# Two projections exchanged, one folding of sums and the loads of x moved, in a fused attention kernel

## The chip, the cores and the metric

The kernel runs on one core of one Trainium2 chip. The metric is the device time of one execution in microseconds (us). The kernel before takes 1832.31 us, the median of 3 runs (1831.64 to 1833.32).

## What is computed

For x of shape (32, 256, 32, 32) in float32, with S = 32 x 32 = 1024 tokens per batch element, the reference computes a group normalization, a causal attention with 8 heads of 32 channels that leaves out the diagonal, and a residual addition:

```
xn = gn(x)                                # 32 groups of 8 channels
q  = q_w @ xn + q_b;  kv = kv_w @ xn + kv_b
k, v = kv[:, :256], kv[:, 256:]           # each to (B, 8 heads, S, 32)
scores = q k^T / sqrt(32);  scores = where(mask == 0, -10000, scores)
attn   = softmax(scores);   attn   = where(mask == 0, 0, attn)
x = x + (attn v)                          # mask = tril(ones, -1)
```

## The kernel before, in words

The program is written out in full for 32 batches. A batch has two groups `g` of four heads (128 channels), and each group has six visits, so a batch has N = 12 visits, 0 to 11. The main loop (L700 to L717) runs over all 384 visits. Step i of it issues, in this order: the scores of visit i (`scores`, L339: products of k and q on TensorE into three PSUM tiles `sT`, exponentials on ScalarE into `e` and `eh`, and on GpSimd the masking of the blocks on the diagonal, `mask`, L320, into `diagonal`); the steps listed for i in `at`; then `values` (L399) and `add_keys` (L421) of visit i - 1, which are the products of the exponentials with v on TensorE into `acc`, and the running sums of the exponentials on VectorE; then the steps listed for i in `after`. Where the text says that something is done after visit i, step i of this loop is meant. A period of the loop, 12 steps, is one batch.

Which key blocks a visit needs is written in `PRODUCTS` (L566): visit 2 needs blocks 0 and 1, visit 3 blocks 2, 6 and 7, visit 4 blocks 4, 6 and 5. `projections` (L268) lists twelve pieces of projection per batch in order: eight of q and k (`project_qk`, tiles `pp`) and four of v (`project_v`, tiles `ppv`). Piece n of v, n = 0 to 3, makes the key blocks 2n and 2n + 1, and ends with a copy on ScalarE (L266). `PROJECT` (L621) gives each of the twelve pieces its step relative to the first visit of its batch, -5 to 6, in `at`; places 8 and 9 of the list, which hold v's pieces 2 and 3, go to steps 3 and 4.

Around these pieces other steps are placed by hand:

- `prepare` (L609) with `PREPARE` (L622) places the ten steps of a batch's normalization in `after`: statistics of the two channel groups (`norm_channels`, L172), `norm_mean` (L180, product `pm`), `norm_deviation` (L188, tile `dev` on VectorE), `norm_variance` (L200, product `pv` on `dev`), `norm_rstd`, and the four applications. They stand relative to the batch's first visit, so that -16 is visit 8 of the batch two before, and -9 and -8 are visits 3 and 4 of the batch just before.
- `SUMS` (L623) places the folding of the four sums of exponentials per batch. Sum n is first folded from 128 to 64 partitions (`fold`, L436: a DMA of 512 KB, issued by GpSimd, that adds one half of the tile to the other) in step SUMS[n], then from 64 to 32 (256 KB) two steps later, both in `after`, and is stacked (`stack`, L442: a plain DMA of 256 KB issued by SyncE) four steps after the first, in `at`. A step above 11 lies in the next batch. Sums 0 and 2 lie in `diagonal` tiles, sums 1 and 3 in `e` tiles. In step N + 8 the inverted sums are written to memory and read back into `rb` by four DMAs of 256 KB (`invert`, L485).
- `finish` (L519) divides, adds bias and residual on VectorE and stores each quarter of the output, in steps N + 13 (twice), N + 14 and N + 15.
- The loads of x, four of 256 KB per batch, are listed in `at` (L674).

TensorE, ScalarE, VectorE and GpSimd execute their instructions in the order in which this program issues them. On SyncE's queue, which carries the loads, the stackings, the inverses and the stores, a scheduler decides on the order: before the change it is, from visit 7 of one batch to visit 6 of the next: the stacking of sum 0, the write of the previous batch's inverses and the four reads of `rb`, the stackings of sums 1 and 2, the previous batch's four stores, one load of x, the stacking of sum 3, three loads. An instruction waits there for what it needs, and everything behind it waits too.

Of the kernel before, what the change touches and what calls it, by code (L numbers as in the profile page):

```python
# [32 lines left out]
def tile_norm_attention_residual(  # L33
# [24 lines left out]
    NH = S // HALF  # L58
# [40 lines left out]
    def unshifted():  # L99
# [4 lines left out]
        def load_part(b, g, cols):  # L104
            if (g, cols.start) == (0, 0):
                live["x", b] = xpool.tile([P, NG, S], F32, tag="x", name=f"x_{b}")
            nc.sync.dma_start(out=live["x", b][:, g, cols], in_=x_in[b, :, g, cols])
# [129 lines left out]
        def project_qk(b, g, n, hf):  # L237

            key = ("qk"[n], b, g)
            if hf == 0:  # L240
                live[key] = qkpool.tile([P, S], F32, tag="qk"[n], name=f"{'qk'[n]}_{b}_{g}")
            cols = slice(hf * HALF, (hf + 1) * HALF)
            pp = spare(f"pp_{b}_{g}_{n}_{hf}")
            for cc in range(NG):
                product(
                    pp, wT[:, cc, n * C + g * P : n * C + (g + 1) * P], live["xn", b, hf][:, cc, :],
                    start=cc == 0, stop=cc == NG - 1,
                )
            nc.scalar.activation(  # L249
                live[key][:, cols], pp, AF.Identity, bias=qk_bias[:, n, g : g + 1], scale=(SCALE, 1.0)[n],  # L250
            )

        def project_v(b, n):


            if n == 0:
                live["v", b] = work.tile([P, NB, C], F32, tag="v", name=f"v_{b}")
            pp = spare(f"ppv_{b}_{n}").rearrange("p (s c) -> p s c", c=C)
            hf, at = divmod(2 * n * P, HALF)
            for s in range(2):  # L260
                tokens = slice(at + s * P, at + (s + 1) * P)
                for cc in range(NG):
                    product(
                        pp[:, s, :], live["xn", b, hf][:, cc, tokens], wT[:, cc, 2 * C : 3 * C], start=cc == 0, stop=cc == NG - 1,
                    )
            nc.scalar.copy(live["v", b][:, 2 * n : 2 * n + 2, :], pp)  # L266

        def projections(b):  # L268

            qk = [[lambda g=g, hf=hf, n=n: project_qk(b, g, n, hf) for n in range(2)] for g in range(NG) for hf in range(NH)]  # L270
            v = [lambda n=n: project_v(b, n) for n in range(NB // 2)]
            return qk[0] + v[:1] + qk[1][:1] + v[1:2] + qk[1][1:] + qk[2] + v[2:] + qk[3]

# [160 lines left out]
        def fold(b, n, rows):  # L436
            total = live["sum", b, *divmod(n, NH)]
            if (n, rows) == (1, HD):
                nc.gpsimd.drain()
            nc.gpsimd.dma_start(out=total[:rows], in_=total[rows : 2 * rows], accum_op=ALU.add)  # L440

        def stack(b, n):  # L442
            if n == 0:
                live["folded", b] = work.tile([P, 4, HALF], F32, tag="folded", bufs=1, name=f"folded_{b}")
            total = live.pop(("sum", b, *divmod(n, NH)))
            nc.sync.dma_start(out=live["folded", b][n * HD : (n + 1) * HD], in_=total[:HD])

        def sum_folded(b, heads):
            if heads.start == 0:
                live["rows", b] = small.tile([P, ROW], F32, tag="rows", name=f"rows_{b}")  # L450
            for j in heads:
                turned = small.tile([P, HALF], F32, tag="turned", bufs=1, name=f"turned_{b}_{j}")
                nc.vector.transpose(turned, live["folded", b][:, j, :])
                nc.vector.tensor_reduce(
                    live["rows", b][:, j * HALF // HD : (j + 1) * HALF // HD],
                    turned.rearrange("p (k r) -> p k r", r=HD), AX.X, ALU.add,
                )
# [27 lines left out]
        def invert(b):  # L485
            rows = live["rows", b]
            check(rows, SUM_MIN, SUM_MAX)
            inv = small.tile([P, ROW], F32, tag="inv", name=f"inv_{b}")
            nc.vector.reciprocal(inv, rows)
            turned = small.tile([P, ROW], F32, tag="inv_turned", name=f"inv_turned_{b}")  # L490
            nc.vector.transpose(turned, inv)

            spread = dram.tile([2, 4, 2, HALF], F32, tag="inv", name=f"inverses_{b}")
            nc.sync.dma_start(
                out=spread.rearrange("a n j (m c) -> (n j m) a c", c=HD), in_=turned.rearrange("p (a c) -> p a c", a=2),
            )
            live["rb", b] = work.tile([P, 4, HALF], F32, tag="rb", bufs=1, name=f"rb_{b}")
            for h in range(4):
                nc.sync.dma_start(
                    out=live["rb", b][h * HD : (h + 1) * HD],  # L500
                    in_=spread[h // 2, :, h % 2, :].unsqueeze(0).broadcast_to([HD, 4, HALF]),
                )
# [60 lines left out]
        N, TOTAL = NG * len(VISITS), 2  # L563
# [42 lines left out]
        def when(i, f, where=at):  # L606
            where.setdefault(i, []).append(f)

        def prepare(b, whens):  # L609
            for n, f in zip(whens, [  # L610
                lambda: norm_channels(b, 0), lambda: norm_channels(b, 1), lambda: norm_mean(b),
                lambda: norm_deviation(b), lambda: norm_variance(b), lambda: norm_rstd(b),
            ] + [lambda hf=hf, g=g: norm_apply(b, hf, g) for hf in range(NH) for g in range(NG)]):
                if n is None:
                    f()
                else:
                    when(n, f, after)
# [1 line left out]


        PROJECT = (-5, -4, -3, -2, -1, 0, 1, 2, 3, 4, 5, 6)  # L621
        PREPARE = (-16, -15, -9, -9, -8, -8, -7, -6, -5, -3)  # L622
        SUMS = (3, 7, 9, 13)  # L623
        FINISH = (N + 13, N + 13, N + 14, N + 15)
        every = range(4)

        with tc.manual_schedule(engines={ENG.PE, ENG.Activation, ENG.DVE, ENG.Pool}):
# [38 lines left out]
            for b in range(B):  # L666
                first, last = b * N, b == B - 1
                if b >= 1:
                    for n, f in zip(PROJECT if not last else PROJECT[:-1] + (7,), projections(b)):
                        when(first + n, f)  # L670
                if b >= 2:
                    for n in range(NG * NH):
                        cols = slice(n % NH * HALF, (n % NH + 1) * HALF)
                        when(max(first - 2 * N + 4 + n, 0), lambda b=b, n=n, cols=cols: load_part(b, n // NH, cols))  # L674
                    prepare(b, [first + n for n in PREPARE])
                if not last:
                    for n in every:
                        v = first + SUMS[n]
                        when(v, lambda b=b, n=n: fold(b, n, 2 * HD), after)
                        when(v + 2, lambda b=b, n=n: fold(b, n, HD), after)  # L680
                        when(v + 4, lambda b=b, n=n: stack(b, n))
                    late = b == B - 2
                    v = first + N + (5 if late else 6)
                    when(v, lambda b=b: sum_folded(b, every[:2]), after)
                    when(v + 1, lambda b=b: sum_folded(b, every[2:]), after)
                    when(v + 2, lambda b=b: invert(b))
                    for n in every:
                        v = first + (N + 9 + n // 2 if late else FINISH[n])
                        when(v, lambda b=b, n=n: finish(b, n), after)
                else:  # L690
                    when(first + 3, lambda: sums(0, SUMMED[1], False), after)
                    when(first + 7, lambda: sums(1, SUMMED[5], False), after)
                    when(first + 9, lambda: sums(2, SUMMED[7], False), after)
                    when(first + 8, lambda b=b: invert_here(b, 0))
                    when(first + 9, lambda b=b: finish(b, 0))
                    when(first + 8, lambda b=b: invert_here(b, 1))
                    when(first + 8, lambda b=b: finish(b, 1))
                    when(first + 10, lambda b=b: invert_here(b, 2))
                    when(first + 11, lambda b=b: finish(b, 2), after)
            for i in range(B * N + 1):  # L700
# [4 lines left out]
                b, v = divmod(i - 1, N)  # L705
# [21 lines left out]
    def shifted():  # L727


        with ExitStack() as inner:  # L730
# [34 lines left out]
            with tc.For_i(0, B, 1) as b:  # L765
# [93 lines left out]
                )  # L859

    outside = unshifted()
    again = nc.values_load(outside[0:1, 0:1], min_val=0, max_val=P)
    with tc.If(again > 0):
# [26 lines left out]
```

## Time and profile before

| what | value |
|---|---|
| median of 3 runs | 1832.31 us |
| the profiled execution's own time | 1834.49 us |
| span of the profiled execution, from first to last instruction | 1832.8 us |
| granted TensorE clock | 0.998 |
| TensorE products (PE) | 1800.6 us busy |
| VectorE (DVE) | 1642.0 us busy, 90% |
| ScalarE (ACT) | 1456.2 us busy, 79% |
| GpSimd (POOL) | 842.1 us busy, 46% |
| DMA queue of GpSimd's folds (q0) | 97.53 MB, 36.0% of 16 engines' span |
| DMA queue of SyncE (q1) | 133.96 MB, 27.3% |
| instruction queue (q8) | 291 packets, 4.77 MB, 1.1% |

A line of a timeline gives start and duration in us, the engine, the line of the kernel, the operation, the tile written and those read, the shape, and a count of merged instructions. A bracket at its end tells how long the engine was idle before and what ended that. A line of the waits gives the waiting instruction, what it waited for, the total in us, how often, and the longest. PE is TensorE's products, PEld its loading of weights. "issue" means a wait for nothing that the profile shows. A line of DMA queues gives the kind of queue, its packets, MB, and the share of the time of 16 DMA engines in the stretch. Names of tiles stand without batch and buffer numbers.

### The profile page before, as it was taken

To read this page: it belongs to the slowest core of one execution; us is meant where nothing else is said; L and a number is where in the kernel's file an instruction comes from. 1 tells how busy PE (TensorE), PEld (TensorE's weight loads), DVE (VectorE), ACT (ScalarE), POOL (GpSimd) and SP (SyncE) were. 2 spreads that over 40 slices of the span, in tenths; PEclk is the share of its full clock that TensorE was granted. 3 is DMA by queue.
4 is the path that set the end of the run, shared out by engine and by line. 5 is a ranking of instruction groups with operands and counts; after the bars stand their busy time and mean duration, and the time that the engine had idled before them with its cause. 6 is when DMAs were issued, how large, how long until landed. Compare 5 with 4: busy or idle time off the path is not lost.

```text
span 1832.8 us, 81736 instructions
## 1 busy us (share of the span) xinstructions
PE 1800.6 (98%) x37036; PEld 958.2 (52%) x37036; DVE 1642.0 (90%) x1832; ACT 1456.2 (79%) x1985; POOL 842.1 (46%) x901
## 2 busy tenths in 40 slices
PE   9999999999999999999999999999999999999997
PEld 5555555555555555555555555555555555555553
DVE  4688999999998998999999999999998999999987
ACT  6778778888778887787887888877878778888774
POOL 2444544545544454445454454554444544545531
PEclk9999999999999999999999999999999999999999
DMA  3456676776766766666667666666666676766662
GB/s 122 72 101 136 128 142 122 136 151 120 145 124 129 144 135 126 132 132 135 143 128 148 116 135 147 127 137 126 138 135 130 132 142 124 136 146 124 123 123 74
DMA packets 86531, 236.79 MB, mean 129 GB/s; under 512 B 21280, under 2 KB 22304, under 8 KB 70304
## 3 DMA queue, kind: packets, MB, share of 16 engines
q0 software_dynamic: 15872, 97.53, 36.0%
q1 hardware_dynamic: 70304, 133.96, 27.3%
q8 instruction: 291, 4.77, 1.1%
q14 instruction: 64, 0.52, 0.1%
HBM read 66.85 MB, written 34.57 MB: 55 GB/s over the span
## 4 chain that ended last, share of the span: by engine, by line
PE 92%; ACT 6%; issue 1%; DVE 1%; DMA 0%; POOL 0%
PE sT L302 30%; PE pp L162 26%; PE acc L409 26%; PE ppv L162 10%; ACT e L384 3%; ACT eh L380 2%; ACT v L266 1%; PE pd L461 0%; DMA x<-in_x_dram 0%; PE pv L162 0%; DVE st L177 0%; PE pm L162 0%; POOL diagonal L330 0%; DVE rb_last L526 0%; DVE rb_last L514 0%
## 5 line engine op out<-in xcount | busy, mean ns | idle before, releaser
L384 ACT ACTIVATE e<-sT 128x1024 f32<-128x1024 f32 x768 | 745.6, 1022 | 263.1 <-PE sT L302 262.9
L330 POOL TENSOR_SCALAR_AFFINE_SELECT diagonal<-eh 128x512 f32<-128x512 f32 x512 | 541.6, 1081 | 777.9 <-ACT eh L380 777.8
L302 PE MATMUL sT<-q,k 32*64 32x128 f32 (+2 forms) x18432 | 587.7, 372 | 4.7 <-issue 4.4
L427 DVE TENSOR_TENSOR e<-e,e 128x1024 f32<-128x1024 f32 x315 | 541.9, 1720 | 19.5 <-ACT v L266 3.2
L302 PEld LDWEIGHTS sT<-q,k 32*64 32x64 f32 x18432 | 405.6, 131 | 188.8 <-PE sT L302 59.5
L162 PE MATMUL pp<-xn,wT 128*32 128x512 f32 x4096 | 493.2, 598 | 1.3 <-ACT e L384 1.1
L409 PE MATMUL acc<-e,v 128*32 128x384 f32 (+3 forms) x4608 | 402.0, 450 | 0.0
L380 ACT ACTIVATE eh<-sT 128x768 f32<-128x768 f32 (+1 forms) x384 | 341.0, 888 | 0.0
L409 PEld LDWEIGHTS acc<-e,v 128*32 128x32 f32 x4608 | 149.7, 110 | 261.1 <-issue 238.1
L162 PE MATMUL ppv<-wT,xn 128*32 128x256 f32 x4096 | 247.5, 382 | 0.0
L162 PEld LDWEIGHTS pp<-xn,wT 128*32 128x32 f32 x4096 | 107.8, 109 | 200.1 <-issue 165.6
L427 DVE TENSOR_TENSOR diagonal<-diagonal,e 128x1536 f32<-128x1536 f32 x126 | 188.0, 1492 | 25.7 <-PE acc L409 10.6
L427 DVE TENSOR_TENSOR e<-e,eh 128x1024 f32<-128x1024 f32 x127 | 171.5, 1351 | 6.9 <-ACT q L249 0.5
L409 PEld LDWEIGHTS acc<-diagonal,v 128*32 128x32 f32 x4096 | 119.5, 110 | 108.6 <-issue 97.1
L409 PE MATMUL acc<-diagonal,v 128*32 128x128 f32 x4096 | 160.4, 273 | 12.5 <-ACT v L266 12.5
L427 DVE TENSOR_TENSOR e<-e,diagonal 128x2048 f32<-128x2048 f32 x62 | 142.1, 2292 | 24.1 <-POOL diagonal L330 20.7
L162 PEld LDWEIGHTS ppv<-wT,xn 128*32 128x32 f32 x4096 | 120.4, 109 | 79.6 <-issue 7.2
L427 DVE TENSOR_TENSOR e<-e 128x512 f32<-128x512 f32 x64 | 66.9, 1046 | 80.3 <-PE acc L409 79.6
L526 DVE SCALAR_TENSOR_TENSOR rb<-num,v_bias_col,x 128x256 f32<-128x256 f32 x248 | 133.5, 579 | 4.4
L235 ACT ACTIVATE xn<-x,shift,rstd 128x256 f32<-128x256 f32 x248 | 137.2, 613 | 0.0
L440 POOL DMA_DIRECT2D diagonal<-diagonal x124 | 120.0, 968 | 32.9 <-DMA diagonal<-diagonal 32.4
L440 POOL DMA_DIRECT2D e<-e x124 | 102.3, 825 | 38.1 <-PE sT L302 34.8
(78 smaller groups left out, 1077.0 us busy)
## 6 DMA issues: line engine op xcount, KB each, us to landing
diagonal<-diagonal POOLq DMA_DIRECT2D x62, 512.0 KB, 8.9
e<-e POOLq DMA_DIRECT2D x62, 512.0 KB, 5.7
rb<-inverses SPq DMA_DIRECT2D x124, 256.0 KB, 4.7
out_dram<-rb SPq DMA_DIRECT2D x124, 256.0 KB, 5.0
x<-in_x_dram SPq DMA_DIRECT2D x120, 256.0 KB, 6.0
diagonal<-diagonal POOLq DMA_DIRECT2D x62, 256.0 KB, 4.7
folded<-diagonal SPq DMA_DIRECT2D x62, 256.0 KB, 3.5
e<-e POOLq DMA_DIRECT2D x62, 256.0 KB, 5.4
```

The source lines that it names most:

```text
L162: nc.tensor.matmul(out[part], lhsT=lhsT[:, part], rhs=rhs, start=start, stop=stop, skip_group_check=True)
L235: nc.scalar.activation(to, of, AF.Identity, bias=live["shift", b][:, g : g + 1], scale=rstd)
L266: nc.scalar.copy(live["v", b][:, 2 * n : 2 * n + 2, :], pp)
L302: return nc.tensor.matmul(bank[c : c + KEYS, cols], lhsT=live["k", b, g][rows, kb * P + c : kb * P + c + KEYS], rhs=live["q", b, g][rows, ...
L330: nc.gpsimd.affine_select(out=square[:, :, place + s * P : place + (s + 1) * P], in_=raw[:, :, (1 - s) * KEYS : (3 - s) * KEYS], pattern=[ ...
L380: exp = nc.scalar.activation(eh.rearrange("p (n bank) q -> p bank n q", n=2)[:, :, :, :narrow], short[:, :, :, :narrow], AF.Exp)
L384: nc.scalar.activation(e[:, 2 * a : 2 * a + 2, :wide], pairs[a][:, :, :wide], AF.Exp)
L409: nc.tensor.matmul(acc[HD * j : HD * (j + 1), of], lhsT=live["v", b][:, kb, h * HD : (h + 1) * HD], rhs=e[:, j, :], start=first, stop=last ...
L427: nc.vector.tensor_add(to, to, tile_of(b, g, at))
L440: nc.gpsimd.dma_start(out=total[:rows], in_=total[rows : 2 * rows], accum_op=ALU.add)
L526: nc.vector.scalar_tensor_tensor(blocks(rb, s), blocks(num, s, s == 1), v_bias_col[:, g : g + 1], blocks(xt[:, g, cols], s), ALU.add, ALU.add,
```

## The change

A slice, three numbers and a formula are edited. In the list of projections v's pieces 2 and 3 exchange places, so that piece 3 (key blocks 6 and 7) is made in step 3 and piece 2 (blocks 4 and 5) in step 4. The statistics of x move from -16 and -15 to -14 and -13, from visits 8 and 9 to 10 and 11. The folding of sum 2 moves from step 9 to 11, and with it its second fold from 11 to 13 and its stacking from 13 to 15; steps 13 and 15 are visits 1 and 3 of the next batch. The four loads of x are listed in steps 7, 7, 7 and 8 of the batch two before instead of 4, 5, 6 and 7.

```diff
-            return qk[0] + v[:1] + qk[1][:1] + v[1:2] + qk[1][1:] + qk[2] + v[2:] + qk[3]
+            return qk[0] + v[:1] + qk[1][:1] + v[1:2] + qk[1][1:] + qk[2] + v[:1:-1] + qk[3]
...
-        PREPARE = (-16, -15, -9, -9, -8, -8, -7, -6, -5, -3)
-        SUMS = (3, 7, 9, 13)
+        PREPARE = (-14, -13, -9, -9, -8, -8, -7, -6, -5, -3)
+        SUMS = (3, 7, 11, 13)
...
-                        when(max(first - 2 * N + 4 + n, 0), lambda b=b, n=n, cols=cols: load_part(b, n // NH, cols))
+                        when(max(first - 2 * N + 7 + n // 3, 0), lambda b=b, n=n, cols=cols: load_part(b, n // NH, cols))
```

As built, the order on GpSimd's queue differs only in the two folds of sum 2: the first stands behind the mask of visit 11 instead of behind the second fold of sum 1 in visit 9, the second between the mask of visit 1 and the first fold of sum 3. On SyncE's queue the stacking of sum 2 stands behind the first two stores instead of ahead of all four, and the four loads of x stand together behind the stacking of sum 3.

## The prediction

> **What bounds the kernel now.** I read the page first (busy shares and the chain), then the waits of TensorE, then its timeline in one batch, then VectorE's timeline of the same stretch, last the DMA queues.
>
> ```profile
> PE 1800.6 (98%) x37036; PEld 958.2 (52%) x37036; DVE 1642.0 (90%) x1832; ACT 1456.2 (79%) x1985; POOL 842.1 (46%) x901
> ...
> PE 92%; ACT 6%; issue 1%; DVE 1%; DMA 0%; POOL 0%
> ```
>
> TensorE is busy for 98% of the span and holds 92% of the chain. A change that removes no products can only take away TensorE's stalls, so I list these.
>
> ```profile
> PE acc L409 <- ACT v L266: 12.5, 32, 0.4
> PE sT L302 <- issue: 4.4, 5, 1.8
> ```
>
> The first row is the wait that the exchange of the projections is about: in each of the 32 batches the products of visit 3 wait for ScalarE's copy of the projection issued just ahead of them. The second row has no releaser. Matmul ends are modelled, so I price stalls by distances of starts. TensorE's timeline of two visits with the same products (visit 9 of batch 15 without, visit 3 of batch 16 with the wait; then `pv`, norm_variance):
>
> ```profile
> 913.34 1.04 PE L409 MATMUL acc<-e,v 128*32 128x512 f32 x8
> 914.20 0.62 PE L409 MATMUL acc<-diagonal,v 128*32 128x128 f32 x16
> ...
> 940.97 1.04 PE L409 MATMUL acc<-e,v 128*32 128x512 f32 x8
> 942.40 0.64 PE L409 MATMUL acc<-diagonal,v 128*32 128x128 f32 x16 [0.39 <-ACT v L266]
> 942.83 0.25 PE L162 MATMUL pv<-dev,avg 128*32 128x2 f32 x8
> ```
>
> The start distance is 0.86 us without and 1.43 us with the wait: it costs 0.57 us. VectorE in the same stretch:
>
> ```profile
> 932.90 3.09 DVE L427 TENSOR_TENSOR diagonal<-diagonal,e 128x1536 f32<-128x1536 f32 x2 [0.27 <-issue]
> ...
> 936.63 1.69 DVE L526 SCALAR_TENSOR_TENSOR rb<-num,v_bias_col,x 128x256 f32<-128x256 f32 x2
> ...
> 941.29 0.88 DVE L526 SCALAR_TENSOR_TENSOR rb<-num,v_bias_col,x 128x256 f32<-128x256 f32 x2
> ...
> 942.47 0.16 DVE L197 TENSOR_TENSOR dev<-dev,mv 128x2 f32<-128x2 f32 x1
> ```
>
> This is what the reader should not miss: `dev` ends at 942.63, and `pv` needs it 0.20 us later. From 932.90 to there VectorE is never idle. At the start, for batch 0's own statistics, TensorE does wait for `dev`: it ended at 8.39 and `pv` started at 8.54, so the least lag is 0.15 us, and `pv` can come only 0.05 us earlier; this wait stands right behind the one removed. The lag is 0.20 us in each of batches 2 to 30; in batch 1 it is 2.45 us.
>
> The second thing is the length of a batch, from one `pm` product (norm_mean) to the next:
>
> ```profile
> 655.18 0.22 PE L162 MATMUL pm<-mv,avg 128*32 128x2 f32 x8
> ...
> 713.08 0.22 PE L162 MATMUL pm<-mv,avg 128*32 128x2 f32 x8
> ...
> 937.58 0.22 PE L162 MATMUL pm<-mv,avg 128*32 128x2 f32 x8
> ...
> 993.42 0.22 PE L162 MATMUL pm<-mv,avg 128*32 128x2 f32 x8
> ```
>
> One takes 57.90, the other 55.84 us. Of the 29 such periods, 16 take 55.83 to 55.84 and 13 are longer by 0.06 to 2.06; the excesses sum to 10.4 us. In every batch that I compared the excess arises 37 to 46 us after `pm`, at the turn to the next batch, in mid-scores:
>
> ```profile
> 692.74 1.36 PE L302 MATMUL sT<-q,k 32*64 32x128 f32 x49
> 695.92 0.44 PE L302 MATMUL sT<-q,k 32*64 32x128 f32 x15 [1.82 <-issue]
> ```
>
> The DMA queues from 687.6 to 693.3, just ahead of this stall:
>
> ```profile
> q0 software_dynamic: 127, 0.79, 78.5%
> q1 hardware_dynamic: 78, 0.29, 21.6%
> ```
>
> All 16 engines are full, and no instruction packet is among them. The instruction queue (291 packets of 16 KB on the page) sends one every 6 us; here one started at 681.5, the next only at 693.3, and TensorE resumed at 695.92. In the period that begins at 937.58 the same pair stood at 963.7 and 973.5, 9.8 us apart, with no stall. So TensorE starves once a gap passes about 9.8 us. What fills the engines are the four reads of `rb` (1 MB) and two folds issued together by POOL after visit 9, 256 KB and 512 KB (911.87 and 912.44 in batch 15).
>
> **What the Trainium skill says.** "Runtime: NRT & Kernel Launch", Instruction fetch mechanics: a sequencer streams its program in blocks of 16 KiB, 256 instructions, over a DMA queue of its own, "mostly hidden". The trace agrees on the size (4.77 MB in 291 packets) and differs on the hiding. "DMA: Bandwidth & Descriptors", Queues, rings and completion order: each DMA engine takes its queues in turn, switching between packets. If so, a fetch waits for little; here it starts after most or all of the folds' packets. "SBUF — State Buffer", SBUF: two separate sides: VectorE with two SBUF inputs and a GpSimd operation that reads SBUF lock each other out. The trace agrees: the pair at 936.63, beside a mask (936.64, 1.40 us), took 1.69 instead of 0.88 us.
>
> **The change part by part.**
>
> Projections exchanged. The same 16 products each, in the same two visits; only which tokens. The block for keys 6 and 7 now comes a visit earlier, that for 4 and 5 is first read in visit 4, after its copy of visit 4's start has had a whole visit. Removed: 32 x 0.57 = 18.2 us. In 29 batches (2 to 30) `pv` follows in that visit and takes back all but 0.05: 29 x 0.05 = 1.5 us stays. Batches 0 and 31 have no `pv` there and batch 1 has its `dev` early: 3 x 0.57 = 1.7. Together 3.2 us. Ends of this: 18.2 if `dev` came earlier, 0 if later. Nothing ahead of `dev` on VectorE between 932.90 and 942.63 is moved, so I keep 3.2.
>
> Folding of sum 2. Its 512 KB fold leaves visit 9 for 11, its 256 KB fold leaves 11 for 13 (visit 1 of the next batch), its stacking on SP leaves 13 for 15. POOL's order shows three groups: after visit 9 only one fold of 256 KB stays; after visit 11 one of 512 instead of 256 KB; after visit 1 one of 256 KB ahead of the 512 KB one. In the first place the engines' queue behind the `rb` reads falls from 768 to 256 KB. The pair ran about 5.8 us, a 256 KB fold alone about 2.7, so the fetch comes some 3 us sooner; the longest gap was 11.9, and 11.9 - 3.1 is under 9.8. Gain: the whole 10.4 us; its bounds are 0 and 10.4. At visit 11 the fold runs alone and ends ahead of the next fetch: 0.
>
> At visit 1 lies the cost. The stretch 926.4 to 936.1, between two fetches of batch 16, is already crowded:
>
> ```profile
> q0 software_dynamic: 80, 0.52, 35.1%
> q1 hardware_dynamic: 322, 0.76, 25.9%
> ```
>
> That gap is 9.7 us with a 512 KB fold and two stores, and now 256 KB more stand ahead. If the fetch waits for everything, its gap grows by 2.7 us and TensorE starves 2.6 us per batch; if it waits for some four packets per engine, as most of the late fetches at visit 9 did (about 3.6 us after the folds began), it starts no later than now: 0. A stall here falls between `pm` and `pv`, where TensorE now has 0.52 us to spare per batch (0.57 - 0.05), so only what exceeds 0.52 costs. Bounds: 0 and 30 x 2.1 = 63 us. I take 0.1 net per batch, 3 us, since the fetch's request falls after the new fold has begun, with part of the queue already gone.
>
> POOL. The two folds at visit 1 take 0.85 us each after the mask that ends at 929.59; the next mask is at 936.64, so nothing is queued behind. The second fold of sum 2 waits for the first, issued near 920.4 and, with 8.9 us to landing, down near 929.5: bound 0 to 1 us, covered by the same idle time. SP. The stacking of sum 2 now stands behind the first two stores and ahead of the last two; it needs the fold, landed near 935, and the third store is ready at 938.3: 0. If the fold came 3 us late, stores would wait, and they have no reader until the next `rb` read.
>
> Statistics of x. Two steps of 1.28 + 0.21 = 1.49 us go from visits 8 and 9 to 10 and 11. VectorE works without a break from 899.99 to 926.45 and then idles 1.61 before the add at 928.06, which waits for TensorE; the steps stay inside this stretch, so its end doesn't move. They now lie beside other masks; the lock costs up to 0.8 us, below the 1.61. Cost 0; if the cover were gone, `dev` and `pv` would slip by the same amount in each batch.
>
> Loads of x. On SP all four stand together behind the stacking of sum 3 instead of around it, so they go out near 945 instead of 942.6 to 949, land in 6.0 us, and are read 25 us later: 0.
>
> Sum, against the profiled execution's span: 1832.8 - 3.2 - 10.4 + 3.0 = 1822.2. Its own time was 1834.49, 1.7 above its span, so 1823.9; the median of the runs is 2.2 below that time: **1821.7 us**.
>
> **Rivals.**
> (1) *The stall moves to visit 1 and grows.* One mechanism: the 256 KB fold delays the instruction fetch there in every batch. At a delay of 1.3 us the net stall is 0.7, so 21 us: 1832.3 - 13.6 + 21 = 1839.7. It decides from a net stall of 13.6 / 30 = 0.45 us on. For it: the gap of 9.7 is at the limit, and some late fetches at visit 9 waited for the whole of the folds. Against: most didn't, and 0.52 us are absorbed.
> (2) *The fetch stalls stay at visit 9*, since the `rb` reads alone hold the engines; only the projections' 3.2 us come: 1829.1, within what can be told from no change. For it: 1 MB of reads lies in that gap. Against: batches with the same reads and an earlier fetch don't stall.
> (3) *The whole of the 18.2 us comes*, if `dev` isn't what I think: 1832.3 - 18.2 - 10.4 = 1803.7. Against: the constant lag of 0.20.
>
> **How the numbers follow.** Forecast 0.58 (own range 1818 to 1828), rival 1 0.21, rival 2 0.17, rival 3 0.04. A measurement of this kernel can tell some 0.2% (3.7 us) from no change. Faster: 0.58 + 0.04 = 0.62; same 0.17; slower 0.21. The range goes from 1817 to 1838: it leaves out rival 3 and the upper half of rival 1.
>
> **What would show it.** Right: no wait `acc <- ACT v` is left except at the start; a wait of `pv` for `dev` near 0.5 us in 29 batches takes its place; periods near 55.8 without excess at 37 to 46 us after `pm`; at visit 1 the instruction packet stays within 9.8 us of the last. Wrong: gaps of 11 us at visit 1 with a stall in the scores of visit 3 or 4 (rival 1); excesses where they were (rival 2); `pv` without a wait and periods near 55.3 (rival 3).

## The result, and the profile after

The changed kernel takes 1830.09 us (median of 12 runs, 1826.76 to 1833.26), the kernel before beside it 1832.89 us: ratio 0.9981, 95% interval 0.9970 to 0.9991. That is 2.8 us by the medians and 3.5 by the ratio, a third of the 10.6 us forecast. The profiled execution took 1833.26 us with a span of 1831.6, 1.2 less than before; granted clock 0.997. It is the slowest of the twelve, 3.2 us above their median, so the trace that is read here may hold more stall than a usual run.

The page of the changed kernel, busy times and chain:

```profile
PE 1801.3 (98%) x37036; PEld 961.8 (53%) x37036; DVE 1639.0 (89%) x1832; ACT 1456.0 (79%) x1985; POOL 877.6 (48%) x901
...
PE 88%; DVE 9%; issue 2%; ACT 0%; DMA 0%; POOL 0%; DVEq 0%
```

ScalarE has left the chain (6% before), VectorE holds 9% of it (1%), and "issue" has doubled. TensorE's waits say why:

```profile
PE ppv L162 <- issue: 8.4, 9, 1.9
PE pv L162 <- DVE dev L197: 6.3, 19, 0.4
...
PE acc L409 <- issue: 2.2, 2, 1.9
...
PE sT L302 <- issue: 0.3, 1, 0.3
```

The 32 waits of `acc` for ScalarE's copy are gone. A wait of `pv` for `dev` stands in 18 batches (the nineteenth is the program's start), and the waits without a releaser have moved from the scores (4.4 us before) to the projections of v. First the new wait, TensorE's timeline in batch 16, then VectorE's:

```profile
944.38 1.04 PE L409 MATMUL acc<-e,v 128*32 128x512 f32 x8
945.24 0.62 PE L409 MATMUL acc<-diagonal,v 128*32 128x128 f32 x16
946.18 0.24 PE L162 MATMUL pv<-dev,avg 128*32 128x2 f32 x8 [0.33 <-DVE dev L197]
```

```profile
944.69 0.88 DVE L526 SCALAR_TENSOR_TENSOR rb<-num,v_bias_col,x 128x256 f32<-128x256 f32 x2
...
945.88 0.16 DVE L197 TENSOR_TENSOR dev<-dev,mv 128x2 f32<-128x2 f32 x1
```

The two groups of products start 0.86 us apart, as in a visit without the wait (1.43 before). `dev` ends at 946.04, `pv` starts 0.14 us later, which is the least lag of the prediction within 0.01. Now the lengths of batches, four `pm` products of the timeline:

```profile
372.67 0.22 PE L162 MATMUL pm<-mv,avg 128*32 128x2 f32 x8
...
431.24 0.22 PE L162 MATMUL pm<-mv,avg 128*32 128x2 f32 x8
...
941.00 0.22 PE L162 MATMUL pm<-mv,avg 128*32 128x2 f32 x8
...
996.77 0.22 PE L162 MATMUL pm<-mv,avg 128*32 128x2 f32 x8
```

An undisturbed period takes 55.77 us (55.83 to 55.84 before), the first of these 58.57. I number the periods from 0 in the order of the loop, so that period 6 begins at 431.24; where the expectations below speak of batch n, they mean period n. Of periods 1 to 28, 16 are undisturbed; the excesses of the other 12 sum to 14.3 us (10.5 before). Of the old kind, 37 to 46 us after `pm`, 0.4 us is left. 12.3 us arise in the first 12 us after `pm`, in visits 4 and 5: each of periods 2 to 10 loses 0.2 to 3.3 us there, and no later one. I call these the stalls at visit 1, after the folds issued there; TensorE itself stands three visits later. The last 1.7 us stand in visits 6, 8 and 9 of periods 20 and 25. TensorE just after the `pm` of 431.24:

```profile
431.39 1.55 PE L302 MATMUL sT<-q,k 32*64 32x256 f32 x48
432.87 1.06 PE L162 MATMUL ppv<-wT,xn 128*32 128x256 f32 x12
435.65 1.27 PE L162 MATMUL ppv<-wT,xn 128*32 128x256 f32 x18 [1.72 <-issue]
```

And the DMA queues from 421.7 to 433.1, between two instruction packets (they start at 420.7 and 433.2, 12.5 us apart):

```profile
q0 software_dynamic: 128, 0.79, 53.4%
q1 hardware_dynamic: 331, 0.76, 21.4%
...
out_dram<-rb SPq DMA_DIRECT2D x3, 256.0 KB, 8.2
e<-e POOLq DMA_DIRECT2D x1, 512.0 KB, 9.0
diagonal<-diagonal POOLq DMA_DIRECT2D x1, 256.0 KB, 4.5
```

No packet of the instruction queue q8 is among them (one packet of 8 KB belongs to another, q14). The fold of sum 2 (`diagonal`, 256 KB) and that of sum 3 (`e`, 512 KB) run together with the stores and the stacking, and TensorE stands until 2.4 us after the next packet's start. The page counts 290 packets on q8 against 37036 products and as many weight loads, which is some 255 of TensorE's recorded instructions to a packet. By these counts a packet of q8 carries a block of TensorE's program; I call the place in the program where a block ends its border. A batch has 2304 recorded instructions, close to nine blocks, so by this estimate each batch meets the borders at nearly the same places. At visit 9, where the 512 KB fold left, the stretch between two packets looks like this (968.6 to 976.1, packets at 967.6 and 976.0, 8.4 us apart):

```profile
q1 hardware_dynamic: 576, 1.05, 68.9%
q0 software_dynamic: 46, 0.26, 23.5%
q8 instruction: 1, 0.02, 1.0%
```

So 10 us came from visit 9 and 5 from the exchange with the two ends of the program; new stalls took 14 back, 12 of these at visit 1. Lengths by part, from the start to the first `pm` of the loop, the 29 periods, and from the last `pm` to the end: 93.5 + 1629.7 + 109.6 before, 92.5 + 1631.4 + 107.7 after.

### The profile page after: what moved, and what is told of

The parts are those of the page before. It is cut to its first block, busy times and chain, and to the rows that moved or that the text cites. A ratio compares the mean times of both kernels' runs of the same rounds, so it can differ in the third digit from the quotient of the medians.

```text
span 1831.6 us, 81672 instructions
## 1 busy us (share of the span) xinstructions
PE 1801.3 (98%) x37036; PEld 961.8 (53%) x37036; DVE 1639.0 (89%) x1832; ACT 1456.0 (79%) x1985; POOL 877.6 (48%) x901
## 4 chain that ended last, share of the span: by engine, by line
PE 88%; DVE 9%; issue 2%; ACT 0%; DMA 0%; POOL 0%; DVEq 0%
PE sT L302 27%; PE pp L162 26%; PE acc L409 24%; PE ppv L162 10%; DVE diagonal L427 3%; DVE e L427 2%; DVE rb L526 2%; DVE num L524 1%; PE pd L461 0%; PE pv L162 0%; ACT e L384 0%; DMA x<-in_x_dram 0%; DVE dev L197 0%; DVE dev L196 0%; DVE rb L531 0%
## 5 line engine op out<-in xcount | busy, mean ns | idle before, releaser
L330 POOL TENSOR_SCALAR_AFFINE_SELECT diagonal<-eh 128x512 f32<-128x512 f32 x512 | 580.8, 1157 | 768.2 <-ACT eh L380 765.7
L162 PE MATMUL ppv<-wT,xn 128*32 128x256 f32 x4096 | 252.8, 383 | 8.4 <-issue 8.4
L427 DVE TENSOR_TENSOR diagonal<-diagonal,e 128x1536 f32<-128x1536 f32 x126 | 187.9, 1492 | 25.8 <-PE acc L409 10.6
L427 DVE TENSOR_TENSOR e<-e,eh 128x1024 f32<-128x1024 f32 x127 | 179.2, 1411 | 6.5
L409 PEld LDWEIGHTS acc<-diagonal,v 128*32 128x32 f32 x4096 | 124.6, 110 | 86.1 <-issue 73.1
L440 POOL DMA_DIRECT2D e<-e x124 | 111.5, 899 | 75.5 <-issue 38.2
L427 DVE TENSOR_TENSOR e<-e 128x512 f32<-128x512 f32 x64 | 62.6, 978 | 72.6 <-PE acc L409 72.6
L440 POOL DMA_DIRECT2D diagonal<-diagonal x124 | 111.6, 900 | 0.2 <-issue 0.2
```

The costliest lines, as they stand in the source:

```text
L162: nc.tensor.matmul(out[part], lhsT=lhsT[:, part], rhs=rhs, start=start, stop=stop, skip_group_check=True)
L330: nc.gpsimd.affine_select(out=square[:, :, place + s * P : place + (s + 1) * P], in_=raw[:, :, (1 - s) * KEYS : (3 - s) * KEYS], pattern=[ ...
L409: nc.tensor.matmul(acc[HD * j : HD * (j + 1), of], lhsT=live["v", b][:, kb, h * HD : (h + 1) * HD], rhs=e[:, j, :], start=first, stop=last ...
L427: nc.vector.tensor_add(to, to, tile_of(b, g, at))
```

## The experiments

Theory A: the exchange is worth what the wait for `dev` leaves of it; the folding of sum 2 carries both the gain at visit 9 and the loss at visit 1; statistics and loads are worth nothing. Against it stood that the loads or the statistics make the stalls at visit 1. All ratios are to the kernel before. "Excess" is the sum of the periods' lengths over the undisturbed one of that kernel, read from one profiled execution each. Its places are the visits of the loop: visits 4 and 5 reach from `pm` to 10 us after it, visits 6 to 8 from there to 23 us, in an undisturbed period.

**Exchange alone.**

```diff
-            return ... + qk[2] + v[2:] + qk[3]
+            return ... + qk[2] + v[:1:-1] + qk[3]
```

> The kernel before with the exchange of the two projections alone. Theory A (the exchange is worth what the wait of pv for dev leaves of it, some 0.06 us in a batch and 0.57 in three): 3 us less than before, ratio 0.998; no wait of acc for ScalarE's copy, a wait of pv for dev of 0.3 to 0.5 us in some 20 batches; undisturbed periods of 55.77 us; the excesses of the 13 periods at visit 9 stay (10 us). Rival B (pv is not what takes it back, and the small gain of the whole change comes from elsewhere): 15 to 18 us less, ratio 0.991.

Ratio 0.9976 (0.9966 to 0.9986), 4.4 us less; period 55.77, excess 7.3 us, all but 0.2 of it at 37 to 46 us after `pm`. TensorE's waits:

```profile
PE pv L162 <- DVE dev L197: 9.9, 30, 0.4
```

One of the 30 is the program's start; the other 29 are nearly every `pv` of the loop, since no stall at visit 1 takes the place of the wait here. Theory A holds, rival B is out.

**Folding of sum 2 alone.**

```diff
-        SUMS = (3, 7, 9, 13)
+        SUMS = (3, 7, 11, 13)
```

> The kernel before with the folding of sum 2 moved alone (first fold after visit 11, second after visit 1). Theory A (this fold carries both the gain at visit 9 and the loss at visit 1): the excess at 37 to 46 us after pm is gone (10 us less), and a new one of 10 to 15 us in all stands 5 to 10 us after the next pm, in the first third of the batches; together between 2 us less and 6 us more than before, ratio 0.999 to 1.003. Rival C (the stalls at visit 1 come from the packed loads of x or from the moved statistics): 10 us less, ratio 0.9945, no excess after the next pm.

Ratio 1.0186 (1.0158 to 1.0214): 34 us more, far past both theories. The excess at visit 9 is gone as expected; 48 us stand elsewhere, 35 of them in periods 1 to 6, at 4.4 to 9 us each. In these periods the fetch is late twice in a row. TensorE in period 2, which begins at 209.1:

```profile
217.94 1.03 PE L409 MATMUL acc<-e,v 128*32 128x384 f32 x13
222.00 0.30 PE L409 MATMUL acc<-e,v 128*32 128x128 f32 x2 [3.04 <-issue]
...
222.78 2.14 PE L302 MATMUL sT<-q,k 32*64 32x128 f32 x48
```

The packets before this stall started at 199.1, 209.6 and 219.5. Between the last two, from 210.7 to 219.4, the queues carried:

```profile
q0 software_dynamic: 125, 0.79, 66.0%
q1 hardware_dynamic: 357, 0.73, 27.2%
```

That is a second pair of folds, those of visit 3 (256 KB of sum 3, 512 KB of the next sum 0), with the stacking of sum 3 and loads of x behind them. It stands in every kernel here. In the changed kernel's period 6 a packet started at 438.6, 5.4 us after the late one, in spite of it; here the packet of 209.6 had been late behind the first pair, and the next was late behind the second. The stall isn't all of the cost. The 48 products of the last line of TensorE take 2.14 us, where 48 of this shape take 1.48 near the start of the changed kernel: from 223.2 to 226.6 the trace gives a granted clock of 0.50. Such stretches stand behind the long stalls of all six periods, 23.9 us together, so by an estimate of half of that some 12 of the 35 us are TensorE at half clock. The changed kernel has one, 3.4 us long, in period 10.

**Statistics and loads alone.**

```diff
-        PREPARE = (-16, -15, ...
+        PREPARE = (-14, -13, ...
-        when(max(first - 2 * N + 4 + n, 0), ...
+        when(max(first - 2 * N + 7 + n // 3, 0), ...
```

> The kernel before with the moved statistics and loads of x alone, which were costed at nothing. Theory A: within 0.1% of before, the excesses at visit 9 as before. Rival C (they carry the stalls at visit 1): 5 to 14 us more, ratio 1.003 to 1.008, with an excess 5 to 10 us after pm.

Ratio 0.9992 (0.9981 to 1.0004), excess 6.4 us, at visit 9 as before. Rival C is out: on their own they make no stall at visit 1.

**Changed kernel, last quarter of finish later.**

```diff
-        FINISH = (N + 13, N + 13, N + 14, N + 15)
+        FINISH = (N + 13, N + 13, N + 14, N + 16)
```

> The changed kernel with the last of the four quarters of finish moved from step N + 15 to N + 16, so that its 2.9 us of VectorE's work stand behind dev instead of ahead of it. Theory A (dev behind this work is what pv waits for, and nothing else is late in that visit): the wait of pv for dev is gone and the period falls from 55.77 to about 55.3; with 29 batches some 13 us less than the changed kernel, ratio to before 0.991 to 0.992. Rival D (another thing is late right behind: the adds of visit 4 come later by 2.9 us on VectorE, and with them the buffers of the exponentials): between 3 us less and 10 us more than the changed kernel, ratio 0.996 to 1.004, with a wait of the scores or of ScalarE for VectorE instead.

Ratio 0.9944 (0.9926 to 0.9963), half of the gain expected. The wait is gone. VectorE first, then TensorE, in the visit that answers to the one above:

```profile
939.04 0.16 DVE L197 TENSOR_TENSOR dev<-dev,mv 128x2 f32<-128x2 f32 x1
939.12 2.29 DVE L427 TENSOR_TENSOR e<-e,e 128x2048 f32<-128x2048 f32 x1
```

```profile
939.92 0.62 PE L409 MATMUL acc<-diagonal,v 128*32 128x128 f32 x16
940.40 0.24 PE L162 MATMUL pv<-dev,avg 128*32 128x2 f32 x8
```

`dev` now ends 1.2 us ahead of `pv`, and the undisturbed period is 55.31, 0.46 shorter. But the excess rose from 14.3 to 17.7 us. The slack ahead of `pv` had swallowed up to 0.5 us of each stall at visit 1, some 4 us in all, and no longer does; the stalls themselves came out smaller, so that visits 4 and 5 hold 13.2 us instead of 12.3. Another 4.4 us stand in visits 8 and 9, where the changed kernel lost 1.2. Theory A's mechanism holds; its sum left out the absorption and the new stalls.

**Block borders 64 instructions earlier.** The changed kernel, and in `keep_busy`:

```diff
-            for _ in range(n):
-                nc.tensor.matmul(pt[:, 0, :P], lhsT=ident, rhs=ident, ...)
+            for k in range(n):
+                w = P if k < 8 else 4
+                nc.tensor.matmul(pt[:, 0, :w], lhsT=ident, rhs=ident[:, :w], ...)
...
-            keep_busy(16)
+            keep_busy(32)
```

A warming product of the program is two products and two weight loads in the trace, so 16 more are 64 instructions.

> The changed kernel with TensorE's program 64 instructions longer ahead of the first batch, in about the same time: of the 16 warming products at the start, which no output uses, 8 stay and 24 of 4 columns take the place of the other 8 (a product is four instructions). All DMAs and all other work stay where they are; only the borders of the instruction blocks come 64 instructions, some 1.5 us, earlier in the work. Theory A (the stalls at visit 1 hang on where a block ends against the 768 KB of folds; the border drifts earlier from batch to batch, which is why they end with batch 10): batches 2 to 10 now have the borders of batches past 11, so the excess 5 to 10 us after pm, 13 us in the changed kernel, falls below 4 us; 9 to 13 us less than the changed kernel, ratio to before 0.991 to 0.993. Rival E (the early batches stall for another reason, their data or the warming up of something): as the changed kernel within 3 us, ratio 0.996 to 1.0, the same batches stalled.

Ratio 1.0101 (1.0087 to 1.0116). The warming took 8 us longer than meant, since TensorE stayed slow through it (see the last section), and the first `pm` of the loop stands at 101.6 instead of 92.5; less these 9.1 us the span is still 10 us above the changed kernel's (1850.9 - 9.1 against 1831.6). The stalls at visit 1 are gone, as theory A said: nothing is left in visits 4 and 5. In periods 2 to 10 the packet there now starts 1.9 to 3.0 us ahead of `pm`, where in the changed kernel it starts 0.6 to 1.9 us behind it. Yet the excess is 22 us, now 11 to 21 us after `pm`, 20 of it in visit 6 and the rest in visits 7 and 8, and in periods 3 to 5, 11 to 13 and most of those from 18 on. TensorE in one of them:

```profile
1238.73 1.05 PE L163 MATMUL pp<-xn,wT 128*32 128x512 f32 x5
1241.36 1.48 PE L163 MATMUL pp<-xn,wT 128*32 128x512 f32 x10 [1.58 <-issue]
```

The packets stand at 1230.5 and 1239.1. From 1231.5 to 1239.0 the queues carried most of the folds of visit 3 and part of the four packed loads:

```profile
q0 software_dynamic: 110, 0.64, 60.4%
q1 hardware_dynamic: 227, 0.57, 29.6%
...
x<-in_x_dram SPq DMA_DIRECT2D x4, 256.0 KB, 6.7
```

Rival E is out: with the same DMAs and the same work the stalls move with the borders. Theory A's sum is out too, since the borders only met another crowd.

**Block borders 192 earlier.** As above, with 3 full and 61 small warming products (`k < 3`, `keep_busy(64)`).

> As the shift by 64, but by 192 instructions (3 full warming products and 61 of 4 columns), which is 64 short of a whole block, so that the borders come some 1.5 us later in the work than in the changed kernel. Theory A: batches past 10 now have the borders that batches 2 to 10 had, so the excess 5 to 10 us after pm stands in most of the batches, 15 to 40 us in all; 5 to 30 us more than the changed kernel, ratio to before 1.001 to 1.015. Rival E: as the changed kernel within 3 us.

Ratio 1.0457 (1.0439 to 1.0475), more than theory A's range. Of the 77 us of span above the changed kernel's, 23 lie ahead of the first `pm` of the loop, 5 behind the last, and the rest in the periods: their excess is 63 us instead of 14, and 26 of 29 periods are longer than 55.9. That late borders stall nearly every batch is what theory A said; the place isn't: 46 us stand in visit 6, 10 in visit 7 and only 7 in visits 4 and 5. In each of periods 1 to 28 the packet near `pm` starts 0.2 to 2.3 us behind it, after all 0.79 MB of the folds of visit 1, and in 21 of them nearly all of the folds of visit 3 (0.75 MB or more) come ahead of the next one too. So the two crowds follow one another, and TensorE stands at the second.

**Folding and loads.** The edits of the folding and of the loads, on the kernel before:

```diff
+        SUMS = (3, 7, 11, 13)
+        when(max(first - 2 * N + 7 + n // 3, 0), ...
```

> The kernel before with the folding of sum 2 and the loads of x moved as in the change, without the exchange of projections and the moved statistics. With the folding alone the first six batches lost 4 to 9 us each: a late fetch at visit 1 was followed by a second one across the folds of visit 3, with the first load of x in the same stretch. Theory F (the packed loads, which go out behind the stacking of sum 3, take 256 KB out of that stretch and keep the second fetch in time): the large excesses of the first batches fall from 4 to 9 us to 1 to 3, and the time is 0 to 8 us more than before, ratio 1.000 to 1.004. Rival G (the exchange of the projections, with its slack ahead of pv, or the statistics do it): as with the folding alone, 30 to 38 us more than before, ratio 1.016 to 1.021.

Ratio 1.0130 (1.0108 to 1.0152), excess 34 us, 3.3 to 5.4 in each of periods 1 to 6. Theory F explains less than a third of what the whole change gains over the folding alone, and rival G's range is missed as well: the loads help, but they are not what keeps the second fetch in time.

**Folding and exchange.**

```diff
+            return ... + qk[2] + v[:1:-1] + qk[3]
+        SUMS = (3, 7, 11, 13)
```

> The kernel before with the folding of sum 2 moved and the projections exchanged, statistics and loads where they were. The folding alone gave 1.0186, with the loads 1.013, in the whole change 0.998: something else in the change keeps the early batches from stalling twice. Theory G (it is the exchange, which leaves 0.5 us of slack ahead of pv and makes TensorE reach the border a little before the folds of visit 3): ratio 0.998 to 1.005, excess of the first six batches 0 to 3 us each. Rival M (it is the moved statistics, or all three together): ratio 1.010 to 1.018, excess of the first six batches 3 to 9 us each.

Ratio 1.0032 (1.0021 to 1.0044), excess 20 us; five of periods 1 to 6 lose 0.3 to 2.0 us, one 4.9. Theory G holds by its ratio: the exchange alone takes the folding's cost from 34 us down to 10 (over the exchange without it). In the five the packet after the late one starts 7.1 to 7.8 us after `pm`; in the one that lost 4.9 it starts at 10.3, and with the folding alone it starts at 9.7 to 12.8. Why the exchange brings it forward isn't shown: what it changes in TensorE's time there is half a microsecond.

**Changed kernel, folding put back.**

```diff
-        SUMS = (3, 7, 11, 13)
+        SUMS = (3, 7, 9, 13)
```

> The changed kernel with only the folding of sum 2 put back to step 9 (second fold 11, stacking 13). Theory A (the folding's move gave 10 us back at visit 9 and took 13 at visit 1, so in the changed kernel it nets to a small loss; the exchange gives 3, statistics and loads 0): 4 to 6 us less than before, ratio 0.9965 to 0.998, no excess 5 to 10 us after pm, 5 to 10 us of excess at 37 to 46 us. Rival J (the folding's move is a gain in the changed kernel, and without it the time of before comes back but for the 3 us): ratio 0.998 to 0.9995.

Ratio 0.9992 (0.9982 to 1.0003). No excess is left 5 to 10 us after `pm`, but that at 37 to 46 us is 12.4, more than the 10.5 of before and the 7.3 of the exchange alone, so most of the exchange's gain goes there. Against the changed kernel's 0.9981 the move of the folding is a gain of 2 us that the intervals don't tell from none. Neither theory's number is hit cleanly; rival J's range holds it.

**The same with the later finish.**

```diff
+        SUMS = (3, 7, 9, 13)
+        FINISH = (N + 13, N + 13, N + 14, N + 16)
```

> The changed kernel with the folding of sum 2 back at step 9 and the last quarter of finish at N + 16. Theory A: the later finish takes away the wait of pv for dev, 0.46 us in a batch, and no stall at visit 1 takes it back: 1811 to 1816 us, ratio 0.989 to 0.992. Rival K (the later finish costs elsewhere what the stalls at visit 1 had hidden): ratio 0.994 to 0.996.

1817.39 us, ratio 0.9916 (0.9902 to 0.9930): with the next one the fastest that was run, 15 us below the kernel before and 5 us below the changed kernel with the later finish. Theory A holds by its ratio. TensorE's first wait in it:

```profile
PE sT L302 <- issue: 4.2, 10, 0.7
```

The stalls at visit 9 are many and short (9.9 us of excess). With no slack ahead of `pv`, then, the folding seems better left where it was (0.9916 against 0.9944, the intervals just overlapping).

**Folding at step 10.** The changed kernel with both of these:

```diff
+        SUMS = (3, 7, 10, 13)
+        FINISH = (N + 13, N + 13, N + 14, N + 16)
```

> The changed kernel with the folding of sum 2 at step 10 (second fold 12, stacking 14) and the last quarter of finish at N + 16, so that neither visit 9 nor visit 1 issues two folds together. Theory A (what starves TensorE is two folds together with the stores or the reads of rb): excess at visit 1 below 3 us and at 37 to 46 us below 4, 1805 to 1811 us, ratio 0.986 to 0.989. Rival L (512 KB anywhere near the reads of rb delays the fetch as much as 768): 10 us or more of excess at 37 to 46 us, ratio 0.991 to 0.995.

Ratio 0.9919 (0.9904 to 0.9934), excess 12.7 us, 10 of it at 37 to 46 us after `pm`. Theory A's point that two folds together are what starves TensorE falls: one fold of 512 KB after the `rb` reads, a visit later, does as much. Rival L holds.

**Later finish and 64 instructions.** Both edits on the changed kernel.

> The changed kernel with the last quarter of finish a step later and with the borders of the instruction blocks 64 instructions earlier, both together. Theory A: the two gains add, 6 to 7 us from the later finish with its stalls and 14 more from the stalls at visit 1 (17 us in that run) that go: 1806 to 1812 us, ratio 0.986 to 0.989. Rival E: no more than the later finish alone, ratio 0.993 to 0.996.

Ratio 0.9963 (0.9950 to 0.9976), 1824.72 us, of which 9.2 are the longer start. Both ranges are missed. Visit 4 is clear here as well; of 12.5 us of excess 10 stand in visits 6 to 8 and 2 in visit 5. Without the cost of the start it would be near 1815.5, by subtraction only: the gain that theory A expected, less the new stalls.

## Why the prediction was wrong

Against the profiled execution's span the forecast was -3.2 - 10.4 + 3.0 = -10.6 us; it came to -5.2 - 10.2 + 14.1 = -1.3, against the 1.2 measured.

1. *Exchange, 3.2 us.* The mechanism was right. The undisturbed period fell by 0.065 us (28 x 0.065 = 1.8), the first period by 0.5 without its excess, and the two ends of the program by 2.9, together 5.2; alone it gave 4.4 (2.6 to 6.2). `dev` behind the last quarter of `finish` on VectorE is what takes the rest: with that quarter a step later the period lost another 0.46.
2. *Excess at visit 9, 10.4 us.* Right in this execution: 10.5 fell to 0.3 or 0.4. As a price it is softer than it looked, since the same fold in the same place left 6.4, 7.3 and 12.0 us in three kernels that differ elsewhere.
3. *Visit 1, 3 us.* This is the step that failed: the net cost of the second fold at visit 1. It held that the fetch's request "falls after the new fold has begun, with part of the queue already gone", so 0.1 us net per batch. Ahead of the stalls of periods 2 to 10 the packet instead started after all of the 768 KB of folds (0.79 MB each time), 10.4 to 12.5 us after the one before, at up to 3.3 us each; later periods got theirs at gaps of 8 to 10.5, with 0.48 to 0.73 MB of the folds gone (periods 12 to 26). The term was 12.3 us, or 14.1 with the other new stalls, not 3. The 0.52 us of absorption was right in kind (0.46 by the later finish): in 11 of the 29 batches that wait with the exchange alone no wait of `pv` is left here, nine of them just those stalled at visit 1. What the working lacked is the border of the instruction block as a quantity of its own: I took one batch's spacing for all, while the stalls here began and ended with the number of the batch, and moving the borders by 64 instructions swapped them for others. In the trace the packet ahead of the crowd starts 46.6 us after `pm` in period 1, 45.5 in period 8 and 44.7 in period 11, so the borders seem to drift against the work.
4. *Statistics, loads, SyncE, 0.* Right for the statistics and loads by themselves. A cost of zero added to the rest was still too simple: the median store took 7.6 us to land instead of 5.0 and the stacking from `diagonal` 6.0 instead of 3.5, with no reader late, but all of it shares the engines that the fetch needs. With the exchange beside them the two came with 0.9992 against 0.9976 for the exchange alone, 3 us that the overlapping intervals don't settle, and the fold's price ran from +34 us alone to -2 among the other parts.

Rival 1 named what happened, the stall at visit 1 in the work right behind it, and set its deciding point at 0.45 us net per batch, close to which the run came (12.3 / 30 = 0.41, or 14.1 / 30 = 0.47). It expected the same stall in every batch; a third of them have it. Rival 2 ended near the measured time by the wrong road: the stalls at visit 9 did go. That 1830.09 us still lies inside the outer range of 1817 to 1838 is no merit of the sum. Open is why the exchange protects the early batches from the second late fetch, and what decides on a packet's place behind the others.

## What to carry to other kernels

Before a bulk DMA is moved on a core whose TensorE is almost never idle, list the gaps between instruction packets in every batch and treat each crowded stretch as a place where the next block may come late; moving the load elsewhere can only move the stall unless it lands in a real lull. Where a wait is removed, look for what is late right behind it and move that as well: the exchange alone gave 4 us, with `finish` a step later and the folding left alone (statistics and loads moved) 15. Test such parts together, since the parts of this change did not add.

## What the runs showed that I had not expected

- A shift of the program by 64 or 192 instructions, with all DMAs in place, moved 12 us of stalls from visits 4 and 5 to visits 6 to 8, where they came to 22, or raised the excess from 14 to 63 us.
- A single edit of two folds cost 34 us, by letting two late packets follow each other: 4.4 to 9 us per period where one late packet costs 0.2 to 3.3. Part of this is no stall: behind the stalls of 1.9 to 4.3 us there the granted clock was 0.50 for 3.4 us, once for 6.8. It isn't so behind every such stall; with 192 instructions one of 2.8 us went without.
- Warming products of 4 columns saved no time: 64 of TensorE's products at the start, 48 of them with 4 columns, took 13.81 us, 0.22 us each, against 5.42 us for 32 with 128 columns, 0.17 each. The 32 start 0.21 us apart in their first half and 0.11 in their second; the 64 stay at 0.21 to the end, and six with 128 columns soon after them took 1.47 us instead of 0.83. So TensorE was slower in that stretch for products of either width. Whether the narrow ones are the reason wasn't tried apart.
